# Degree-sorted neighbours, a stride-26 node layout and one maxima scheme for every head group in a two-layer graph kernel

## The chip, the cores and the metric

The kernel runs on one core of a Trainium2 chip. The core has a matrix engine (PE, with its weight loads listed as PEld), a vector engine (DVE), an activation engine (ACT), a general engine (POOL) and a queue engine (SP) that issues most of the transfers. Each works through its own instructions in order. The metric is the device time of one execution in microseconds (us); less is better.

## The reference

There are 3327 nodes with 128 features and a sparse matrix `adj` of about five entries a row, self-loops included. The second layer is the expensive one.

```python
# layer 0
x = layernorm(x + (A/rowsum(A)) @ x @ W_in + (A.T/rowsum(A.T)) @ x @ W_out)
# layer 1: N = 3327 nodes, 128 "heads" of 8 components each
q, k, v = [(x @ W.T).reshape(128, N, 8) for W in (Wq, Wk, Wv)]
a = einsum('dnh,dmh->dnm', q, k) * 128**-0.5
a = softmax(a + adj + adj, axis=2)            # 128 matrices of N x N
out = einsum('dnm,dmh->dnh', a, v)
x = layernorm(x + out.reshape(N, 1024) @ Wo.T)
```

The reshape cuts the flat row of q, k and v: head d holds the flat entries d*N to (d+1)*N.

## The kernel before

It never adds `adj` to the N x N scores. It makes a softmax without `adj` for all keys, makes the few neighbour terms apart, and joins the two at the end. Fewer than 17 entries a row have to be nonzero; a proof made on the way (`worst`, `crowd`, `short`, `outside`) decides at the end whether a general and much longer second path (`general_maxima`, `general_sums`) must run instead.

**Before the main loop.** Layer 0 reads `adj` and its transpose, and the vector engine takes each row's 16 largest entries (`weight`, `where`). Then 13 rounds of projections write q, k and v to DRAM: in three bf16 parts for the matmuls (`q_d`, `k_d`) and in f32 (`qf_d`, `kf_d`, `v_d`). The squared length of each key goes to `size_d` and that of each query to `reach_d` (ACT square, DVE reduction, L660 to L664). For the first 32 heads `early_of` selects the 2048 longest keys of a head (`select`), packs them with one-hot matmuls (`fills`, tile `hot`), and spreads them into `k_kept`.

**The main loop** goes over 32 groups of four heads (`GH`), seven blocks of up to 512 queries (the last has 255), and 26 tiles of 128 keys. A step is one key tile: two "halves" of two heads each. A half is a pair of matmuls of 50 rows, 24 key rows twice over and two rows that add the negated maximum (`e_ps`, L1241), and one exp of 128x1024 (`es`, L1259; L1261 in the last block, where one half does four heads). Each step ends with the eight f32 matmuls of four heads' weighted sums (`o`, L1192). A full group is 338 halves, 312 of them L1259.

**The side streams** are woven into these halves by a hand-written order (`tc.manual_schedule`), so that what an engine does next is fixed at build time.

- The *maxima* that a softmax needs come from `stream_of`, one "item" at a time: two matmuls into two of three PSUM banks (L1001) and two DVE reductions (L1010). Groups 1 to 31 use two levels. `of_top` takes 26 query tiles against the 1024 longest keys, 52 items for each pair of heads; `fix` finds by `reach * top_least > best**2` at most 8 queries a partition that need more, gathers them on POOL (`slot_each`, L816 to L826, then `slot_parts`); `of_rest` runs those against the next 1024 keys, 18 items; `merge` joins both. Group 0 uses `of_block`: every query against all 2048 keys, 208 items. `to_queries` transposes the result and stores it in four pieces per block (`negmax_d<-turned`, L938) and copies it to `flatmax_d` (L942).
- `due` says how many items must be out at which half; an item goes out where it is behind. 49 items (`LEAD`) go out ahead of the first half. Up to half 310 (`READY`) the rate is almost an item a half, and about one in two later.
- `choices` runs `select` for the other 96 heads, from half 310 on (DVE, L421 to L530).
- `by_node` copies k and v into tables by node (`kn_d`, `vn_d`), one transfer of 26 nodes each, every sixth half up to half 1536 (`START`).
- `neighbours` goes from half 1536 on over 26 tiles of 128 nodes (node = 128*t + p). For each of 16 slots it gathers a neighbour's k row (L1041) and takes 128 dot products on DVE (`dots`, L1076 and L1080); after an exp, 16 v rows are gathered, weighted and added on POOL (L1145, L1146). Query rows and results move in pieces of 32 nodes by SP (`transfer`, L1070). It may advance only where the estimated work of DVE and POOL (`credit`) leaves room.

The transfers of the maxima's and the exp's operands are queued in `coming` and go out on SP one per half (`begin_next`, L387); a block's own are forced out when it begins. Keys are laid out by tile and partition as t*128 + p, so that `v4`, `whole_q` and `reach_of` are loaded in pieces of 36, 32 and 4 bytes.

**After the loop** `last` joins both softmax parts, multiplies by Wo and normalizes.

Of the kernel before, what the change touches and what calls it, by code (L numbers as in the profile page):

```python
# [9 lines left out]
F32 = mybir.dt.float32  # L10
# [15 lines left out]
H = 8  # L26
# [15 lines left out]
SLOTS = 16  # L42
EPS = 1e-5
# [3 lines left out]
QUARTER = 32  # L47
STRIPE = 26
START = 1536
LEAD = 49  # L50
TURN = 5
# [16 lines left out]
READY = 310  # L68
# [12 lines left out]
def gnn_layers(ctx: ExitStack, tc: tile.TileContext, x, adj, adjt, w_in, w_out, wq, wk, wv, wo, out):  # L81
# [34 lines left out]
    near = const.tile([P, NT, SLOTS], U32, name="near")  # L116
    weight = const.tile([P, NT, SLOTS], F32, name="weight")
    gain = const.tile([P, NT, SLOTS], F32, name="gain")
# [12 lines left out]
    vn_d = dram.tile([N, HEADS * H], F32, name="vn_d")  # L131
    ones_d = dram.tile([2, NP], BF16, name="ones_d")
    x1_d = dram.tile([NP, D], F32, name="x1_d")
    size_d = dram.tile([G], F32, name="size_d")
    reach_d = dram.tile([G], F32, name="reach_d")
# [3 lines left out]
    negmax_d = dram.tile([NG * len(BLOCKS), 2, GH * NB], BF16, name="negmax_d")  # L139
# [23 lines left out]
    with ExitStack() as c0:  # L163
# [4 lines left out]
        with ExitStack() as c1:  # L168
# [14 lines left out]
            nc.gpsimd.dma_start(near_d[HEADS * N :, :].rearrange("(o g) w -> o g w", o=1), zeros)  # L183
            nc.gpsimd.dma_start(
# [3 lines left out]
            big = c1.enter_context(tc.tile_pool(name="big", bufs=1))  # L188
            rows = c1.enter_context(tc.tile_pool(name="rows", bufs=6))
# [89 lines left out]
            nc.vector.tensor_copy(near, where)  # L279
            with tc.tile_pool(name="ps_mix", bufs=2, space=PSUM) as ps_mix:  # L280
# [16 lines left out]
                nc.vector.tensor_reduce(over, used, axis=AX.X, op=ALU.add)  # L297
                nc.vector.tensor_tensor(over, over, count, op=ALU.not_equal)
                nc.vector.tensor_scalar(below, below, -1.0, 0.0, op0=ALU.mult, op1=ALU.max)
# [9 lines left out]
        early = c_att.enter_context(tc.tile_pool(name="early", bufs=1))  # L309
        hot_no = early.tile([P, 2 * REACH], BF16, name="hot_no")  # L310
# [11 lines left out]
        def load_group(g):  # L322
# [9 lines left out]
            for j in range(GH):  # L332
                at = (g * GH + j) * N
                pairs.append((v4[:, j, :, :], v_d[at : at + NP, :].rearrange("(t p) w -> p t w", p=P)))
# [13 lines left out]
        def load_queries(what, g, b):  # L348
# [5 lines left out]
            for y in range(2):  # L354
                for slot, part in enumerate(QROWS):
                    r = 64 * (y if what == "e" else 1 - y) + H * slot
                    src = q_d[part * H : (part + 1) * H, at : at + GH * N].rearrange("h (x y n) -> y h x n", y=2, n=N)[y]
                    pairs.append((q[r : r + H, :, :wp], src[:, :, :wp]))
            chunk = negmax_d[g * len(BLOCKS) + b]
            for y in range(2 if what == "e" else 0):  # L360
                pairs.append((q[64 * y + KR : 64 * y + KR + 2, :, :], chunk.rearrange("a (x y n) -> y a x n", y=2, n=NB)[y]))
# [47 lines left out]
        def select(pool, bank, first, n, tag=""):  # L409
# [11 lines left out]
            nc.sync.dma_start(sizes[: P - 1], flat[:, :whole].rearrange("h (p t) -> p h t", t=NT))  # L421
# [181 lines left out]
        with ExitStack() as c1:  # L603
# [9 lines left out]
            def early_of(first, n, g):  # L613
# [4 lines left out]
                packed = chooser.tile([P, KEPT], BF16, name="packed", bufs=2)  # L618
# [9 lines left out]
                spread(g, packed)  # L628

            choosing = [(early_of(*EARLY[0], 0), 1, 8), (early_of(*EARLY[1], 1), 4, 9)]  # L630
            for t in range(NT // 2):
# [4 lines left out]
                for s in range(2):  # L636
                    for name in ("wq", "wk", "wv"):
# [20 lines left out]
                        square = stage.tile([P, H, D], F32, name="square", bufs=1)  # L658
                        scale = 0.5 * D**-0.5 if name == "wq" else 1.0
                        nc.scalar.activation(square.rearrange("p h c -> p (h c)"), pr, AF.Square, scale=scale)  # L660
                        size = stage.tile([P, D], F32, name="size")
                        nc.vector.tensor_reduce(size, square.rearrange("p h c -> p c h"), axis=AX.X, op=ALU.add)
                        to = reach_d if name == "wq" else size_d
                        nc.gpsimd.dma_start(to[g].rearrange("(p s c) -> p s c", p=P, s=2)[:, s], size)  # L664
# [28 lines left out]
    with c_att as c1:  # L693
# [21 lines left out]
        def fills(g, at, parts):  # L715
            packed = side.tile([P, KEPT], BF16, name="packed")
            for u in range(TCUTS):
                state = {}
                tiles = tiles_of_fill(u)
                yield "hots", g, at, tiles[0], state  # L720
                for t, after in zip(tiles, [*tiles[1:], None]):
                    yield "fill", g, at, parts, packed, u, t, after, t == tiles[0], state
# [4 lines left out]
        def of_block(b):  # L727

            ntl = -(-BLOCKS[b][1] // P)
            mx = work.tile([P, NB // P, GH, KCUTS], F32, name="mx_block")  # L730
            q = queries_of("b", 0, b)
            begin_all(("b", 0, b))
            if b + 1 < len(BLOCKS):
                queries_of("b", 0, b + 1)
            for i in range(ntl):
                for x in range(2):
                    for c in range(KCUTS):
                        yield "maxima", 0, q[:, x, :], mx, i, i, x, c, 2 * x
            running.append(after_block(b, ntl, mx))

        def after_block(b, ntl, mx):
            yield
            most = work.tile([P, GH, NB // P], F32, name="most_block")
            nc.vector.tensor_reduce(
                most[:, :, :ntl], mx[:, :ntl].rearrange("p i j c -> p j i c"), axis=AX.X, op=ALU.max
            )
            two = work.tile([P, 2, GH, NB // P], BF16, name="two_block")
# [818 lines left out]
```

## Time and profile before

| | |
|---|---|
| median of 3 runs | 13527.34 us (13521.73 to 13539.56) |
| profiled execution, its own time | 13491.75 us |
| its span | 13490.0 us |
| granted PE clock, mean | 0.922 |
| busy share of the span | PE 86%, ACT 81%, DVE 73%, POOL 34% |
| first exp of the main loop, last one's end | 1080.8 us, 13226.2 us |
| DMA packets, of these under 512 bytes | 3442249, 3104237 |

A line of a group reads: source line, engine, operation, output and inputs with their shapes, count | busy time, mean duration in ns | idle time of the engine just before, and what ended it. A line of waits reads: who waited, for whom, us in all, times, longest. A line of a window reads: start and end in us, length, busy time of the engine with its number of instructions, granted PE clock, share of DMA in use, GB/s. The chain is the work that ended last, followed back. "SPq" is SP issuing a transfer; its duration holds the time that the queue made it wait.

### The profile page before, as it was taken

What the parts mean: (1) busy time and instruction counts of PE and PEld (TensorE: products, weight loads), DVE (VectorE), ACT (ScalarE), POOL (GpSimd) and SP (SyncE); (2) the same over time, 40 slices, a digit from 0 to 9 for tenths busy, and PEclk for the clock granted to TensorE, in tenths of its full rate; (3) what the DMA queues carried; (4) which work ended last, traced back from release to release, by engine and by line L of the source; (5) the groups of instructions that cost most, each with busy time, mean ns of one, the idle gap of its engine ahead of it and who ended that gap; (6) DMA issues with size and microseconds to landing.
All of it is one profiled execution on the core that took longest, in us unless ns stands there. A gap on an engine that the chain in (4) does not pass through costs nothing.

```text
span 13490.0 us, 241141 instructions
## 1 busy us (share of the span) xinstructions
PE 11609.4 (86%) x90040; PEld 2857.1 (21%) x90072; DVE 9913.6 (73%) x19323; ACT 10989.4 (81%) x11667; POOL 4541.7 (34%) x4468
## 2 busy tenths in 40 slices
PE   7558878779988889989989899988899899888985
PEld 3221112112221222222222222211222222211113
DVE  9688867667777777777777877777777777778626
ACT  6345767768988889989888899988899899888993
POOL 0120111011444334444432444333444443243454
PEclk8768989889999999999999999999999999999996
DMA  6563344433344445434443344444434444443466
GB/s 236 151 164 30 31 34 35 30 27 44 68 68 63 60 64 74 73 65 68 62 54 58 61 64 71 62 61 66 72 68 69 61 69 63 56 67 57 75 82 132
DMA packets 3442249, 949.64 MB, mean 70 GB/s; under 512 B 3104237, under 2 KB 3285989, under 8 KB 3434407
## 3 DMA queue, kind: packets, MB, share of 16 engines
q1 hardware_dynamic: 3306151, 417.22, 30.6%
q0 software_dynamic: 130176, 470.37, 12.7%
q10 hardware_dynamic: 4736, 46.52, 1.0%
q8 instruction: 710, 11.63, 0.4%
q14 instruction: 476, 3.90, 0.1%
HBM read 780.63 MB, written 156.90 MB: 69 GB/s over the span
## 4 chain that ended last, share of the span: by engine, by line
PE 36%; ACT 24%; DVE 14%; issue 10%; SPq 9%; DMA 7%; POOL 1%; ACTq 0%; DVEq 0%; POOLq 0%
ACT es L1259 21%; PE o L1192 17%; PE e_ps L1241 11%; PE m L1001 4%; SPq L387 4%; DVE mx_top L1010 3%; DVE hot L569 2%; ACT es L1261 1%; DMA reach_of<-reach_d 1%; DMA negmax_d<-turned 1%; DMA near_d<-acc 1%; SPq L777 1%; PE acc L232 1%; SPq L1070 1%; DMA k_kept<-packed 1%
## 5 line engine op out<-in xcount | busy, mean ns | idle before, releaser
L1259 ACT ACTIVATE es<-e_ps 128x1024 f32<-128x1024 f32 (+1 forms) x9984 | 9508.8, 1026 | 1492.2 <-PE e_ps L1241 1376.7
L1192 PE MATMUL o<-es,v 128*9 128x512 f32 x46592 | 5926.1, 581 | 38.1 <-ACT es L1261 9.8
L1010 DVE TENSOR_REDUCE mx_top<-m 128x1 f32<-128x512 f32 x6448 | 4128.9, 684 | 1545.6 <-PE m L1001 1474.0
L1241 PE MATMUL e_ps<-q_e,k_st 50*128 50x512 bf16 (+1 forms) x23296 | 4399.3, 378 | 293.0 <-ACT es L1259 120.3
L1241 PEld LDWEIGHTS <-k_st 50*128 50x128 bf16 (+1 forms) x23296 | 1403.8, 96 | 6893.6 <-issue 6272.2
L1001 PE MATMUL m<-k_kept,q_m 48*128 48x512 bf16 x6448 | 1387.5, 387 | 553.8 <-DMA k_kept<-packed 346.4
L1010 DVE TENSOR_REDUCE mx_rest<-m 128x1 f32<-128x512 f32 x1984 | 1273.0, 684 | 453.5 <-PE m L1001 448.0
L569 DVE TENSOR_SCALAR hot<-hot_no,at 128x336 bf16<-128x336 bf16 x3840 | 1265.0, 393 | 250.8 <-PE m L578 231.3
L1041 POOL DMA_INDIRECT near_rows<-kn_d,near x416 | 402.7, 968 | 2774.7 <-DVE prod L1076 2495.5
L816 POOL TENSOR_TENSOR slot_each<-hits,whole_q 128x832 f32<-128x832 f32 x248 | 409.1, 1650 | 2510.9 <-DVE hits L801 2061.7
L1192 PEld LDWEIGHTS o<-es,v 128*9 128x9 f32 x46592 | 696.6, 89 | 1828.7 <-issue 1477.2
L1146 POOL TENSOR_TENSOR acc<-acc,prod 128x1024 f32<-128x1024 f32 x390 | 907.6, 2327 | 30.6
L1261 ACT ACTIVATE es<-e_ps 128x1020 f32<-128x1020 f32 x832 | 832.3, 1021 | 83.9 <-PE e_ps L1241 50.9
L1145 POOL TENSOR_TENSOR prod<-near_rows,s 128x1024 f32<-128x1024 f32 x390 | 772.2, 1980 | 6.8
L1041 POOL DMA_INDIRECT near_rows<-vn_d,near x416 | 410.4, 987 | 542.2 <-DVE prod L1076 464.3
L1001 PE MATMUL m<-k_kept,slot_rows_q 48*128 48x512 bf16 x1984 | 428.5, 391 | 178.9 <-DVE mx_rest L1010 178.5
L1076 DVE TENSOR_TENSOR prod<-qn,near_rows 128x512 f32<-128x512 f32 x832 | 572.8, 692 | 3.5 <-POOL acc L1146 3.5
L1080 DVE TENSOR_REDUCE s<-prod 128x64 f32<-128x512 f32 x832 | 558.7, 675 | 0.0
L578 PE MATMUL m<-hot,parts 128*24 128x168 bf16 (+9 forms) x7200 | 327.9, 232 | 125.5 <-DVE hot L569 124.6
L1001 PEld LDWEIGHTS <-q_m 48*128 48x128 bf16 x6448 | 334.8, 98 | 395.1 <-DMA k_kept<-packed 339.0
L232 PE MATMUL acc<-a_t,x 128*128 128x512 f32 (+1 forms) x728 | 311.3, 584 | 63.9 <-DMA a_t<-in_adj_dram 43.7
L1010 DVE TENSOR_REDUCE mx_block<-m 128x1 f32<-128x512 f32 x416 | 257.0, 681 | 38.4 <-DMA q_b<-q_d 19.8
(287 smaller groups left out, 6278.8 us busy)
## 6 DMA issues: line engine op xcount, KB each, us to landing
q_m<-q_d SPq DMA_DIRECT2D x744, 52.0 KB
q_e<-q_d SPq DMA_DIRECT2D x2304, 16.0 KB
a_t<-in_adj_dram ACTq DMA_DIRECT2D x13, 1663.5 KB
a_t<-in_adj_dram SPq DMA_DIRECT2D x13, 1663.5 KB
a_t<-in_adjt_dram SPq DMA_DIRECT2D x13, 1663.5 KB
a_t<-in_adjt_dram ACTq DMA_DIRECT2D x13, 1663.5 KB
q_d<-parts SPq DMA_DIRECT2D x13, 1536.0 KB
k_d<-parts SPq DMA_DIRECT2D x13, 1536.0 KB
```

The costliest lines, as they stand in the source:

```text
L569: nc.vector.tensor_scalar(hot, hot_no, at[:, t, j : j + 1], None, op0=ALU.is_equal)
L1001: nc.tensor.matmul(banks[y], of[rows[y], i * P : (i + 1) * P], kept[rows[y], x, c * NB : (c + 1) * NB], start=True, stop=True,)
L1010: nc.vector.tensor_reduce(mx[:, n, j + y, c - c0 : c - c0 + 1], banks[y], axis=AX.X, op=ALU.max)
L1041: nc.gpsimd.indirect_dma_start(rows.rearrange("p d h -> p (d h)"), None, table, bass.IndirectOffsetOnAxis(ap=near[:, t, i : i + 1], axis=0))
L1076: nc.vector.tensor_mul(both[:, d], left[:, d], right[:, d])
L1080: nc.vector.tensor_reduce(to[:, d], both[:, d], axis=AX.X, op=ALU.add)
L1145: nc.gpsimd.tensor_mul(prod, vg, share)
L1146: nc.gpsimd.tensor_add(acc[:, :, :H], acc[:, :, :H], prod)
L1192: nc.tensor.matmul(o[32 * j : 32 * j + VW, :w], v4[:pt, j, t, :], e[j][:pt], start=t == 0, stop=t == NT - 1,)
L1241: nc.tensor.matmul(bank[:pt, y, x * NB // per : x * NB // per + w], k[r, x0 + x, t * P : t * P + pt], q[r, x0 + x, :w], start=True, stop=True,
L1259: nc.scalar.activation(es[:pt, :, :w], bank[:pt, :, :w], AF.Exp, scale=2.0)
L1261: nc.scalar.activation(es[:pt].rearrange(shape, x=per)[:, :, :, :w], bank[:pt].rearrange(shape, x=per)[:, :, :, :w], AF.Exp, scale=2.0,)
```

## The change

Neighbours: the nodes of a partition are sorted by their number of neighbours (`key`, `ranked_key`, `node`), slots and weights are regathered in that order (`info_d`), and the tile of rank t has `CAPS[t]` slots, 211 in all where there were 416. More neighbours than that count as a failed proof. Query rows are gathered by node from a table of their own (`qn_d`), results are scattered to `nn_d`, and 256 transfers turn `nn_d` into `near_d` at the end of the stream. The tables have stripes of 13 nodes, one transfer every third half, and the stream starts at half 3000.

Layout: the node of partition p and tile t is 26*p + t for `v4`, `whole_q` and the maxima, so that these are loaded and stored in one piece a partition, and the matmuls take their stationary operand with a step of 26 elements. The transposes of `to_queries` go; `merge` stores the whole group at once. `reach` is made on POOL from `whole_q` (`prepare`), and `reach_d` goes, with the squares of q.

Maxima: group 0 runs `of_top` and `of_rest` like the others, and all of its 140 items go out ahead of the first half. `fills` follow `of_top(g, 1)` directly, and `of_rest(g, 0)` comes behind them. The large load of `select` is cut into pieces of 8 heads with eight turns between them.

```diff
+CAPS = [16, 14, 12, 11, 11, 10, 10, 9, 9, 8, 8, 8, 8, 7, 7, 7, 7, 7, 6, 6, 6, 5, 5, 5, 5, 4]
-STRIPE = 26
-START = 1536
-LEAD = 49
+STRIPE = 13
+START = 3000
-READY = 310
+READY = 500
...
+                nc.vector.scalar_tensor_tensor(key[0], over, 32.0, tile_no, op0=ALU.mult, op1=ALU.subtract)
+                for r in range(0, 32, 8):
+                    nc.vector.max(ranked_key[:, r : r + 8], key[1])
+                    nc.vector.max_index(found_at[:, r : r + 8], ranked_key[:, r : r + 8], key[0])
+                    nc.vector.match_replace(key[1], ranked_key[:, r : r + 8], key[1], -1.0e9)
...
+                nc.vector.tensor_tensor(key[0], ranked_key[:, :NT], caps, op=ALU.is_gt)
+                nc.vector.tensor_add(over, over, key[0])
...
-                pairs.append((v4[:, j, :, :], v_d[at : at + NP, :].rearrange("(t p) w -> p t w", p=P)))
+                pairs.append((v4[:, j, :, :], v_d[at : at + NP, :].rearrange("(p t) w -> p t w", t=NT)))
...
-            nc.sync.dma_start(sizes[: P - 1], flat[:, :whole].rearrange("h (p t) -> p h t", t=NT))
+            for h in range(0, n, 8):
+                some = slice(h, min(h + 8, n))
+                nc.sync.dma_start(sizes[: P - 1, some], flat[some, :whole].rearrange("h (p t) -> p h t", t=NT))
+                for _ in range(8 if tag == "" else 0):
+                    yield
...
+            for t in range(NT):
+                nc.gpsimd.indirect_dma_start(
+                    info[:, t], None, info_d, bass.IndirectOffsetOnAxis(ap=node[:, t : t + 1], axis=0)
+                )
...
-                        square = stage.tile([P, H, D], F32, name="square", bufs=1)
-                        to = reach_d if name == "wq" else size_d
+                        if name == "wk":
+                            square = stage.tile([P, H, D], F32, name="square", bufs=1)
...
+        def prepare(g, x, found):
+            whole_q = side.tile([P, 2, NT, H], F32, name="whole_q", bufs=2)
+            for y in range(2):
+                nc.sync.dma_start(whole_q[:, y], qf_d[at : at + NP].rearrange("(p t) h -> p t h", t=NT))
+            for _ in range(6):
+                yield
+            nc.gpsimd.tensor_mul(squares, whole_q, whole_q)
...
-                for b in range(len(BLOCKS)):
-                    to_queries(g, b, two[:, b])
+                for a in range(2):
+                    nc.sync.dma_start(
+                        to[0, :, :whole].rearrange("j (p t) -> p j t", t=NT), two[: P - 1, a]
+                    )
+                    nc.sync.dma_start(to[:, :, whole:], two[P - 1 :, a, :, : NT - 1])
+                nc.sync.dma_start(flatmax_d[:, g * GH * N : (g + 1) * GH * N], negmax_d[g])
...
-            for b in range(5):
-                yield from of_block(b)
+            yield from of_top(0, 0)
+            yield from of_top(0, 1)
+            yield from of_rest(0, 0)
+            yield from of_rest(0, 1)
...
                 yield from of_top(g, 1)
+                    parts = split_keys(side, coming_keys[1])
+                    yield from fills(g + 1, coming_keys[0], parts)
                 yield from of_rest(g, 0)
-                    yield from fills(g + 1, coming_keys[0], parts)
                     yield from of_top(g + 1, 0)
...
+            tile_of = slice(i, NP, NT) if of.shape[-1] == NP else slice(i * P, (i + 1) * P)
-                    of[rows[y], i * P : (i + 1) * P],
+                    of[rows[y], tile_of],
...
-                for i in range(SLOTS):
+                for i in range(cap):
...
-            for _ in range(LEAD):
+            while (0, 0) not in stored:
                 for _ in next_item():
                     pass
+                taken += 1
...
-            wanted = [(0, taken), (READY, 2 * KCUTS * NT + 2 * (top + rest))]
+            wanted = [(0, taken), (2 * steps - MARGIN, taken + 4 * top + 4 * rest + 2 * fill + top)]
...
-                                        k[r, x0 + x, t * P : t * P + pt],
+                                        k[r, x0 + x, t:N:NT],
```

## The prediction

> **What bounds the kernel now.** I read the page's totals and chain first, then the windows of the exp (L1259) cut at the group boundaries, the waits, one step of PE, the SP queue, and the groups of two head groups.
>
> ```profile
> PE 11609.4 (86%) x90040; PEld 2857.1 (21%) x90072; DVE 9913.6 (73%) x19323; ACT 10989.4 (81%) x11667; POOL 4541.7 (34%) x4468
> ...
> ACT es L1259 21%; PE o L1192 17%; PE e_ps L1241 11%; PE m L1001 4%; SPq L387 4%; DVE mx_top L1010 3%; DVE hot L569 2%; ACT es L1261 1%; DMA reach_of<-reach_d 1%; DMA negmax_d<-turned 1%; DMA near_d<-acc 1%; SPq L777 1%; PE acc L232 1%; SPq L1070 1%; DMA k_kept<-packed 1%
> ```
>
> PE and ACT are both the busiest and neither is full. In the chain, the entries of SP and DMA (L387, `reach_of`, `negmax_d`, `near_d`, L777, L1070, `k_kept`) add up to some 10%: transfers hold the loop up, not one engine. The windows, with ACT's time in L1259:
>
> ```profile
> 1020.00:1080.80 60.80, 1.28 (x1) 0.50 0.04 9
> 1080.80:1972.00 891.20, 599.75 (x624) 0.95 0.42 34
> 1972.00:3317.30 1345.30, 896.02 (x936) 0.88 0.38 32
> 3317.30:12557.70 9240.40, 7421.86 (x7800) 0.95 0.43 64
> 12557.70:13226.20 668.50, 591.12 (x624) 0.99 0.60 81
> 8113.80:8464.00 350.20, 296.59 (x312) 0.98 0.48 69
> 6972.40:7370.10 397.70, 297.97 (x312) 0.91 0.37 62
> ```
>
> With 312 exps of L1259 a group, these windows hold groups 0-1, 2-4, 5-29, 30-31, then group 18 and group 15 alone. The last two groups, almost without maxima, take 334 us each: ACT paces them. The others take 446, 448 and 370. So the main loop (12,145 us) holds about 32 x 334 = 10,700 us that this change cannot touch and some 1,450 us that wait for something. From the waits, and from the queue of SP:
>
> ```profile
> PE m L1001 <- DMA k_kept<-packed: 346.4, 52, 34.0
> DVE reach_of L786 <- DMA reach_of<-reach_d: 167.5, 30, 16.1
> DVE count_of L448 <- DMA s<-no_size: 132.6, 3, 54.3
> DVE turned L935 <- DMA negmax_d<-turned: 120.0, 42, 11.7
> ...
> 475.92 7.01 SPq L422 DMA_DIRECT2D room<-size_d  x1
> 1969.38 38.41 SPq L422 DMA_DIRECT2D s<-size_d  x1
> 13200.88 28.35 SPq L1070 DMA_DIRECT2D near_d<-acc  x5
> ```
>
> A DVE or PE wait reaches ACT because both run in order: the maxima's reduction is late, its PSUM bank is not free, and the next `e_ps` stands behind that maxima matmul. The SP lines show transfers held in the queue: 38.41 us behind a load of 32x127 pieces, 7.01 behind 4x127, 28.35 for five neighbour pieces ahead of the last `o_d`.
>
> **Before the loop: -20 us.** 26 of the 52 reductions of L662 (1949 ns each) and their squares go: 51 us of DVE work, of which I take half as lying on the chain, -25. The 26 gathers of `info` cost 26 x 0.97 (the row of L1041) = 25 us of POOL, ahead of the first query copies; POOL waits for ACT there, so +5.
>
> **The lead: +187 us.** Before, 60.8 us pass from the first reductions to the first exp. Now group 0's 140 items and about 10 of group 1, during which `merge` takes its turns, come first: 150 x 2 x 684 ns (L1010) = 205 us, with ACT idle. Add 10 us of small DVE operations and 8 us for the last POOL pieces of `fix`, which mostly run beside the 18 items of `of_rest(0, 0)`. The stores of 127 partitions x 4 pieces hold SP like the 4x127 load, twice 7 us, and the queries that carry the maxima come behind them: 25 us. Together 248, less 61.
>
> **Groups 0-1: -125 us.** Group 0 took 1.37 us a half at about 0.9 items a half (565 reductions of L1010 in the 440 us from 1100 on), group 5 took 1.03 at 0.51. Now 396 items fall on 616 halves, 0.64. Between these rows that is 1.14 x 616 + 1.05 x 60 = 766 us against 891.
>
> **Groups 2-4: -135 us.** The three 32x127 loads made DVE wait 132.6 us. Cut in four, each holds SP about 9.5 us (38.4/4), eight turns apart, and DVE finds the data: -115. The other waits go as below, -20.
>
> **Groups 5-29: -480 us**, from four things.
>
> - Waits that end: `k_kept` lands behind `of_rest(g, 0)` instead of just ahead of its use, 346.4/32 = 10.8 us a group; `reach_of` becomes POOL work, 5.2; the `turned` buffers go, 3.8. About -20 a group. Their cover is the 36 halves of `of_rest` and the six turns of `prepare`; without it these 20 us are back.
> - New: the POOL work of `fix(g, 1)`, four pieces of 4.5 us (L816 to L826) and 2 us of `slot_parts`, now runs beside `fills`, and so do the 5.3 us of `split_keys` (L556 to L559). The first `fill` matmul waits for these; behind it on PE stands the next `e_ps`, and ACT behind that. DVE's `hot` suffers beside POOL:
>
> ```profile
> L569 DVE TENSOR_SCALAR hot<-hot_no,at 128x336 bf16<-128x336 bf16 x120 | 29.3, 306 | 5.9 <-PE m L578 5.4
> L569 DVE TENSOR_SCALAR hot<-hot_no,at 128x336 bf16<-128x336 bf16 x120 | 79.2, 728 | 10.0 <-PE m L578 10.0
> ```
>
> The first line is group 18, the second group 15, where the v rows' additions fell on the fills; that group is 47.5 us longer. 26 us of POOL work against the 87 us that the 52 halves of fills took there: 47.5 x 26/87 = 14 us a group. The bounds are 0 and 47. These two items leave -6 x 25 = -150.
> - Six groups like group 15 cost about 230 us over the 350 of a good one. With 211 v rows for 416 about half of that goes: -100.
> - The rest above 350 (9240 - 25 x 350 - 230 = 260 us) sits in lumps of SP: `v4` in 36-byte pieces, `near_d` and `qn` in pieces. All but the tables end: -230. The new copy to `flatmax_d` makes SP wait until the stores of `negmax_d` land, with the next `q_e` pieces queued behind it; these have a block of 50 us to come in, so I set it at nothing, and at 15 us a group if a block ends just then. What is late next is ACT itself.
>
> **Groups 30-31 and the end: -34 us.** 8 us of stalls, and the 28.35 us of neighbour pieces ahead of the last `o_d`, 26. The 256 transfers of `nn_d` are hidden: the 26 x 17 dot-product slots of before took the 26 groups from 4 to 30, so 211 + 26 take 14 to 16 groups from half 3000 (group 9), and the transfers end near group 26. If they came after the loop, each would add the 0.6 us (median) that a table transfer of L1025 holds SP, 150 us in all.
>
> **Strided stationary operands: nothing.** This is the one unknown price. Four lines of PE and one of its loads:
>
> ```profile
> 8308.11 0.39 PE L1241 MATMUL e_ps<-q_e,k_st 50*128 50x512 bf16 x2
> 8308.34 0.38 PE L1001 MATMUL m<-k_kept,q_m 48*128 48x512 bf16 x2
> 8308.76 0.39 PE L1241 MATMUL e_ps<-q_e,k_st 50*128 50x512 bf16 x2
> 8310.06 0.39 PE L1241 MATMUL e_ps<-q_e,k_st 50*128 50x512 bf16 x2
> 8308.34 0.10 PEld L1241 LDWEIGHTS <-k_st 50*128 50x128 bf16 x1
> ```
>
> A pair holds PE 0.23 us, but the second `e_ps` starts 0.42 after `m`: 0.19 us a step are free. Only the load after `o` is exposed, the other two come 0.22 or more ahead. A load of L us then costs (L - 0.10) + 2 x (L - 0.22) - 0.19 a step, which is zero up to L = 0.24. No stationary operand with such a step is in this trace. The nearest row is L662, which reads with a step of 512 bytes: 1949 ns for 1024 elements where twice L1010 is 1368, a factor 1.42. Bounds: 0.10 and 0.14 us, both hidden; I take 0.
>
> The Trainium skill ("SBUF — State Buffer", Door 1: The DMA port swizzle) speaks against this: SBUF has 16-byte lines, and each access that crosses to a new line pays, so bf16 may step at most 8 elements for free; the change steps 26. It gives no size, and no run here shows one. If it doubled the load to 0.20, the sum above would stay as it is.
>
> **The sum.** -20 + 187 - 125 - 135 - 480 - 34 = -607 us, on the profiled execution's own 13,492: 12,885. The median of the runs stands 0.26% above that execution (13,527), so 12,920.
>
> **Rivals.**
>
> - *POOL beside the fills eats the gain.* If the fills slow down in every group as in group 15, by some 30 us instead of 14, groups 5-29 give almost nothing: about 13,330, still 1.5% faster by the first five groups. For it: 728 ns. Against: `credit` keeps the neighbours out while POOL is behind.
> - *No such contention*, if POOL's pieces fall between the `hot`s: 14 x 25 = 350 us more, 12,570.
> - *Slower: the strided loads.* From L = 0.28 us, 2.8 times today's, the formula gives 0.104 us a step, and 5824 steps eat 607 us. At 0.35 it is 0.32 x 5824 = 1,860, so about 14,780. For it: two of three matmul kinds are hit. Against: the factor 1.42.
> - *The second path runs*, because a proof fails. The reference's own adjacency has 5.02 entries a row and 15 at most; sorted by partition the largest per rank are 15, 11, 10, 10, 9, 9, 8, and so on, all within CAPS. Recomputed with the new partitions, the queries that need more than `of_top` number 7 at most, and 8 fit. If it ran, it would repeat the whole loop without the two levels: at least another 12,145 us.
>
> **How the numbers follow.** A difference under 0.2% cannot be told from none here. Forecast 0.67, own range 12,650 to 13,150; POOL contention 0.13 (0.02 of it within 0.2%); no contention 0.10; strided loads 0.08; second path 0.02. So faster 0.67 + 0.11 + 0.10 = 0.88, same 0.02, slower 0.10. The range reaches down to the third case and up over the second, 12,480 to 13,350, and leaves out the slower ones.
>
> **What would show it.** Right: the first exp near 1,250 us; groups 0-1 near 1.13 us a half; `k_kept`, `reach_of` and `turned` gone from the waits; PE loads of L1241 at 0.10 to 0.14 us; no neighbour work in the last five groups; `hot` above 306 ns in every group. Wrong: PE busy all through a step with ACT waiting on `e_ps`, groups 5-29 above 365 us, or a first exp after 1,350.

## The result and the profile after

The changed kernel takes 13,889.46 us (median of 4 runs, 13,886.63 to 13,898.61) against 13,529.28 before: a ratio of 1.0267, 95% interval 1.0249 to 1.0285. It is 2.7% slower. The forecast was 12,920 us, faster. The profiled execution took 13,889.24 us, with a span of 13,887.6.

The page of the changed kernel, with the totals, four rows of the 40 slices (ACT, granted PE clock, DMA share, GB/s) and the chain by line:

```profile
PE 11829.5 (85%) x89960; PEld 3776.2 (27%) x89960; DVE 9298.0 (67%) x17819; ACT 10965.3 (79%) x11599; POOL 3414.8 (25%) x4073
...
ACT  6334888888999999998998999999997333359994
PEclk9767999999999999999999999999999676679997
DMA  6562443443311222222222222222225867851003
GB/s 238 144 158 25 37 37 35 36 37 36 36 20 31 69 66 61 65 62 54 73 60 56 66 55 62 68 56 54 59 64 31 17 17 23 17 21 21 12 7 116
...
PE o L1195 29%; PE e_ps L1244 22%; ACT es L1262 9%; SPq L1151 5%; PE m L1016 5%; DMA near_d<-nn_d 3%; DVE mx_top L1025 3%; PE m L608 1%; SPq L413 1%; DVE hot L599 1%; DVE mx_rest L1025 1%; DMA q_e<-q_d 1%; PE y L1321 1%; DMA k_kept<-packed 0%; ACT o_sb L1204 0%
```

Read the slices from the left: ACT runs at 8 to 9 tenths through most of the loop, better than before, and then drops to 3 for four slices. In the same slices the DMA engines are at 6 to 8 tenths while they move 17 to 23 GB/s, where they moved 54 to 73 GB/s at 2 tenths just before. Something keeps them busy without moving bytes. The windows of the exp (L1262), cut at the group boundaries, measure the hole:

```profile
1229.50:1966.40 736.90, 594.46 (x625) 0.99 0.41 39
1966.40:3112.30 1145.90, 894.57 (x936) 0.95 0.40 36
3112.30:10523.10 7410.80, 6252.19 (x6552) 0.98 0.24 56
10523.10:12290.10 1767.00, 595.10 (x624) 0.70 0.77 20
12290.10:12968.00 677.90, 594.10 (x625) 1.00 0.15 20
12968.00:13638.90 670.90, 590.67 (x624) 1.00 0.05 9
```

These are groups 0-1, 2-4, 5-25, 26-27, 28-29 and 30-31. Groups 26-27 take 1,767 us; the next two take 678. The waits of the changed kernel name what stood in the way, and one line each of the `nn_d` transfers and of the SP queue shows it from the other side (count, then ns min/median/max, first and last start; and start, length):

```profile
ACT es L1262 <- PE e_ps L1244: 1134.2, 680, 121.4
PE e_ps L1244 <- DMA q_e<-negmax_d: 736.9, 13, 135.0
PEld L1244 <- DMA q_e<-negmax_d: 489.1, 6, 133.5
PE e_ps L1244 <- DMA near_d<-nn_d: 242.7, 3, 121.0
PE m L1016 <- DMA k_kept<-packed: 87.6, 4, 58.9
```

```profile
L1151 SPq DMA_DIRECT2D near_d<-nn_d x256: 530/4274/11757, 10587.9 to 12296.1; - x128
```

```profile
11511.84 5.45 SPq L413 DMA_DIRECT2D q_e<-negmax_d  x2
11517.33 62.72 SPq L1151 DMA_DIRECT2D near_d<-nn_d  x11
11580.16 6.95 SPq L413 DMA_DIRECT2D k_kept<-packed  x1
```

All but the last of the 256 transfers that turn `nn_d` into `near_d` fall into groups 26 and 27, as forecast ("the transfers end near group 26"). But one holds SP for a median of 4.27 us, not 0.6; eleven in a row hold it for 62.72 us; and the negated maxima of the next block arrive up to 135 us late. The `k_kept` waits that are left all lie in this stretch too. Without the surplus of 1,767 - 682 = 1,085 us (682 is what groups 26-27 take in the first experiment) the execution would be at 12,800, near the forecast.

### The profile page after: what moved, and what is told of

Same layout as the page of the kernel before. It is cut to its first block, busy times and chain, and to the rows that moved or that the text cites. A ratio compares the mean times of both kernels' runs of the same rounds, so it can differ in the third digit from the quotient of the medians.

```text
span 13887.6 us, 238133 instructions
## 1 busy us (share of the span) xinstructions
PE 11829.5 (85%) x89960; PEld 3776.2 (27%) x89960; DVE 9298.0 (67%) x17819; ACT 10965.3 (79%) x11599; POOL 3414.8 (25%) x4073
## 4 chain that ended last, share of the span: by engine, by line
PE 58%; ACT 10%; SPq 7%; DVE 7%; issue 6%; DMA 6%; POOL 0%; ACTq 0%; another core or an unknown queue 0%; DVEq 0%; POOLq 0%
PE o L1195 29%; PE e_ps L1244 22%; ACT es L1262 9%; SPq L1151 5%; PE m L1016 5%; DMA near_d<-nn_d 3%; DVE mx_top L1025 3%; PE m L608 1%; SPq L413 1%; DVE hot L599 1%; DVE mx_rest L1025 1%; DMA q_e<-q_d 1%; PE y L1321 1%; DMA k_kept<-packed 0%; ACT o_sb L1204 0%
## 5 line engine op out<-in xcount | busy, mean ns | idle before, releaser
L1262 ACT ACTIVATE es<-e_ps 128x1024 f32<-128x1024 f32 (+1 forms) x9984 | 9521.1, 1026 | 2004.5 <-PE e_ps L1244 1134.2
L1025 DVE TENSOR_REDUCE mx_top<-m 128x1 f32<-128x512 f32 x6656 | 4263.2, 685 | 2581.4 <-PE m L1016 2466.9
L1244 PE MATMUL e_ps<-q_e,k_st 50*128 50x512 bf16 (+1 forms) x23296 | 4863.8, 413 | 1188.7 <-DMA q_e<-negmax_d 736.9
L1195 PE MATMUL o<-es,v 128*9 128x512 f32 x46592 | 5830.0, 572 | 33.3 <-ACT es L1264 11.7
L1244 PEld LDWEIGHTS <-k_st 50*128 50x128 bf16 (+1 forms) x23296 | 2198.2, 150 | 7052.2 <-issue 5862.1
L1025 DVE TENSOR_REDUCE mx_rest<-m 128x1 f32<-128x512 f32 x2048 | 1313.8, 685 | 507.7 <-PE m L1016 499.5
L1016 PE MATMUL m<-k_kept,q_m 48*128 48x512 bf16 x6656 | 1447.1, 390 | 207.6 <-DMA k_kept<-packed 87.6
L1016 PEld LDWEIGHTS <-q_m 48*128 48x128 bf16 x6656 | 594.5, 168 | 242.4 <-issue 231.7
L1066 POOL DMA_INDIRECT near_rows<-kn_d,near x211 | 201.0, 953 | 1084.2 <-DVE prod L1076 982.5
L1016 PE MATMUL m<-k_kept,slot_rows_q 48*128 48x512 bf16 x2048 | 432.8, 385 | 17.9 <-DVE mx_rest L1025 14.1
L1138 POOL TENSOR_TENSOR acc<-acc,prod 128x1024 f32<-128x1024 f32 x185 | 432.2, 2336 | 14.5
L1137 POOL TENSOR_TENSOR prod<-near_rows,s 128x1024 f32<-128x1024 f32 x185 | 366.4, 1980 | 2.5
L1009 DVE CAST slot_rows_q<-m 48x512 bf16<-48x512 f32 x256 | 176.3, 689 | 205.9 <-PE m L1000 191.8
L1066 POOL DMA_INDIRECT near_rows<-vn_d,near x211 | 206.8, 980 | 407.0 <-DVE prod L1076 365.4
L840 POOL TENSOR_TENSOR slot_each<-slot_each 128x416 f32<-128x416 f32 x256 | 288.6, 1127 | 20.1
```

What stands on the lines that cost most here:

```text
L1016: nc.tensor.matmul(banks[y], of[rows[y], tile_of], kept[rows[y], x, c * NB : (c + 1) * NB], start=True, stop=True,)
L1025: nc.vector.tensor_reduce(mx[:, i, y, c - c0 : c - c0 + 1], banks[y], axis=AX.X, op=ALU.max)
L1066: nc.gpsimd.indirect_dma_start(rows.rearrange("p d h -> p (d h)"), None, table, bass.IndirectOffsetOnAxis(ap=rows_at, axis=0))
L1138: nc.gpsimd.tensor_add(acc[:, :, :H], acc[:, :, :H], prod)
L1195: nc.tensor.matmul(o[32 * j : 32 * j + VW, :w], v4[:pt, j, t, :], e[j][:pt], start=t == 0, stop=t == NT - 1,)
L1244: nc.tensor.matmul(bank[:pt, y, x * NB // per : x * NB // per + w], k[r, x0 + x, t:N:NT], q[r, x0 + x, :w], start=True, stop=True,)
```

## The experiments

Each kernel is the changed one with the edit shown, except where it says otherwise. The theory: the 256 transfers cost 1,085 us because they move 425,856 pieces of 44 bytes (3,327 nodes x 128 heads), which the DMA engines take slowly. The rivals: their number, their bytes, their place in the kernel, and their queue.

**1. Rows of 64 bytes.**

```diff
-CW = H + 3
+CW = 16
...
-                acc = side.tile([P, HEADS, CW], F32, name="acc", bufs=2)
+                acc = side.tile([P, HEADS, CW], F32, name="acc", bufs=1)
...
+                nc.gpsimd.memset(acc[:, :, H + 3 :], 0.0)
```

> A row of nn_d and near_d is 16 numbers (64 bytes) instead of 11 (44 bytes), the five extra ones zero; acc has one buffer instead of two, for room. Theory 1, the size of the piece: in the changed kernel's profile a 44-byte piece of near_d<-nn_d takes 43 to 49 ns of a DMA engine and a 64-byte or 32-byte piece of other transfers 8 to 10 ns; the 256 last transfers fall to about 0.6 us each on SP, groups 26 and 27 take about 340 to 355 us each instead of 826 and 941, and the time is 13,889 - 1,085 = about 12,800 (12,750 to 12,900). Theory 2, the number of transfers or of pieces, transposed from node order to head order: as many as before, so the time stays at 13,850 to 13,950. Theory 3, the bytes: 64/44 as many, the time rises to 14,300.

Measured: 12,739.32 us, 0.9409 of before (0.9393 to 0.9425). The same two groups and the same transfers in this run:

```profile
10454.30:11136.80 682.50, 594.30 (x625) 0.99 0.55 64
```

```profile
L1152 SPq DMA_DIRECT2D near_d<-nn_d x256: 530/886/3082, 10520.6 to 11132.3; - x128
```

45% more bytes in as many pieces and transfers, and the hole is gone. Theory 1 holds (the time is 11 us below its range); the number of transfers and the bytes are out.

**2. The same transfers, spread out.**

```diff
-                yield
+                for _ in range(2 + n0 // STRIPE % 2):
+                    yield
```

> The same 256 transfers in the same 44-byte pieces, but one for every 2.5 steps of the work beside the loop instead of one for every step: groups 26 to 31 carry them instead of 26 and 27. Theory 1 (the pieces cost some 1,180 us of 16 DMA engines whenever they run, and stop the kernel where they come faster than the engines take them): over about five groups (1,700 us) the engines are 0.7 to 0.8 busy, the loads of negmax and q come through, groups 26 to 31 take 340 to 420 us, the time is 12,850 to 13,250. Rival (each transfer stops the loop by its own, some 4.2 us of lost time, however far apart): the time stays within 60 us of 13,889.

Measured: 13,204.37 us, 0.9752 (0.9736 to 0.9769). The window of groups 26-30:

```profile
10468.30:12628.70 2160.40, 1484.77 (x1560) 0.89 0.57 24
```

Five groups take 2,160 us instead of the 1,694 of experiment 3, a surplus of 466 instead of 1,085. The rival falls. Theory 1's upper end holds for the time, but four of the five groups take 430 to 452 us, not 340 to 420: the pieces are dear here too, and only in part covered. They are also somewhat cheaper: a packet takes 33.3 ns on average, where it takes 44.0 in the changed kernel, and the DMA engines are 0.57 busy.

**3. The same transfers, whole rows.** `near_d` is a straight copy and column H+2 is zero, so the neighbour terms reach the wrong rows: the kernel leaves out the turn from node order to head order.

```diff
-                    near_d[: HEADS * N, :].rearrange("(d n) w -> d n w", n=N)[:, n0 : n0 + n, :],
-                    nn_d[n0 : n0 + n, :].rearrange("n (d w) -> d n w", w=CW),
+                    near_d[n0 * HEADS : (n0 + n) * HEADS, :].rearrange("(n d) w -> n (d w)", d=HEADS),
+                    nn_d[n0 : n0 + n, :],
...
-                nc.gpsimd.tensor_mul(acc[:, :, H + 2], reach, least)
+                nc.gpsimd.tensor_sub(acc[:, :, H + 2], reach, reach)
```

> The 256 last transfers keep their number and their bytes, but near_d is a straight copy of nn_d in whole rows of 5,632 bytes, without the transposition to head order; column H+2 of acc is set to zero by one subtraction so that the last stage takes the same way. The output is therefore not the reference's: the neighbour part goes to the wrong rows. Theory 1 (the pieces of 44 bytes): the transfers cost some 0.3 to 0.6 us each on SP and groups 26 and 27 take 340 to 350 us; the time is 12,780 to 12,850. Rival (the number of transfers, or their place in groups 26 and 27 behind the wait for the last indirect store): 13,700 to 13,950.

Measured: 12,741.27 us, 0.9410 (0.9395 to 0.9426). The transfers and groups 26-27:

```profile
L1151 SPq DMA_DIRECT2D near_d<-nn_d x256: 468/587/1660, 10522.3 to 11124.5; - x128
```

```profile
10457.60:11139.40 681.80, 594.55 (x624) 1.00 0.23 51
```

The bytes, the place and the wait for the last indirect store are as in the changed kernel, so none of them is the cause.

**4. Where a piece begins, or how long it is.** From experiment 1, only 11 of each 16 numbers are carried over; and rows of 48 bytes.

```diff
-                    near_d[: HEADS * N, :].rearrange("(d n) w -> d n w", n=N)[:, n0 : n0 + n, :],
-                    nn_d[n0 : n0 + n, :].rearrange("n (d w) -> d n w", w=CW),
+                    near_d[: HEADS * N, :].rearrange("(d n) w -> d n w", n=N)[:, n0 : n0 + n, : H + 3],
+                    nn_d[n0 : n0 + n, :].rearrange("n (d w) -> d n w", w=CW)[:, :, : H + 3],
...
-        nc.sync.dma_start(n_t, near_d[g, :].rearrange("(p c) w -> p c w", c=D))
+        nc.sync.dma_start(n_t[:, :, : H + 3], near_d[g, : H + 3].rearrange("(p c) w -> p c w", c=D))
```

> As the run with rows of 16 numbers (12,739), but only 11 of each 16 are carried over: pieces of 44 bytes that begin at multiples of 64 bytes on both sides. Theory 'place': a 44-byte piece is dear because its ends lie anywhere, and a piece that begins at a multiple of 64 costs what a whole 64 does: groups 26 and 27 stay at 338 to 350 us, 12,720 to 12,800. Theory 'size': a piece that is no multiple of 32 or 64 bytes is dear wherever it begins: 43 to 49 ns for a piece as in the changed kernel, 13,700 to 13,850.

```diff
-CW = 16
+CW = 12
```

> Rows of 12 numbers (48 bytes, one of them zero) instead of 11 or 16. Theory 'multiples of 64 or 32 alone': 48-byte pieces cost as much as 44-byte ones, 40 to 50 ns, groups 26 and 27 together some 1,700 us, the time 13,750 to 13,900. Theory 'multiples of 16': they cost 10 ns, the time 12,720 to 12,780. In between, should 2 pieces of 4 cost (those that begin off a 64 line on either side by 16 or 48): 20 to 30 ns, 12,800 to 13,250.

Measured: 13,269.22 us, 0.9799 (0.9782 to 0.9815), and 13,587.29 us, 1.0038 (1.0024 to 1.0053). Groups 26-27 of the one and of the other:

```profile
10526.30:11560.40 1034.10, 595.18 (x624) 0.83 0.69 34
```

```profile
10526.70:12002.50 1475.80, 594.67 (x624) 0.73 0.71 25
```

Neither pure theory holds for the first, and none of the three for the second (33.8 ns, above its 20 to 30). The trace's packets say why. The table holds the packets of the transfers' own size that begin in groups 26-27 (97 to 98% of them), and the time of these groups:

| piece | begins at multiples of | mean | median | over 100 ns | groups 26-27 |
|---|---|---|---|---|---|
| 44 bytes (changed kernel) | 44 | 44.0 ns | 11 ns | 6.3%, with 75% of the time | 1,767 us |
| 48 | 48 | 33.8 | 11 | 5.1%, 68% | 1,476 |
| 44 | 64 | 22.4 | 11 | 3.2%, 50% | 1,034 |
| 64 | 64 | 11.3 | 11 | 0.04%, 0.5% | 682 |

Most pieces take 11 ns whatever their size. What is dear is a tail of a few per cent that take 100 to over 800 ns, and of these four rows only that of whole 64 bytes at multiples of 64 is without it. Both place and size count. In the run of 44 bytes of 64, some 110 us more belong to the last stage, which reads `near_d` in 44-byte pieces there (361 us from the last exp to the end instead of 249).

**5. Another queue.** The transfers are issued by POOL, not SP.

```diff
-                nc.sync.dma_start(
+                nc.gpsimd.dma_start(
                     near_d[: HEADS * N, :].rearrange("(d n) w -> d n w", n=N)[:, n0 : n0 + n, :],
```

> The changed kernel, 44-byte pieces, but the 256 last transfers are issued by POOL instead of SP. What it tells apart is where the loads of q_e and negmax_d stand still. If behind the transfers in SP's own order: they come through now; POOL takes the hold instead, some 130 transfers a group at 3.6 us = 470 us beside its own 51 us of work, and fix stands behind that; groups 26 and 27 together 1,000 to 1,100 us instead of 1,767 to 1,821, the time 13,150 to 13,300. If in the 16 DMA engines, which are 0.77 busy with the pieces: a load waits for the same pieces from whatever queue they come, and the time stays within 150 us of 13,889 to 13,952. If POOL's hold decides over fix and with it the maxima: longer than either.

Measured: 13,849.06 us, 1.0240 (1.0223 to 1.0257); groups 26-27 take 1,696 us. The waits of this run, one store of the maxima on SP (start, length), and the two busiest DMA queues of groups 26-27 (packets, MB, share of the 16 engines; q0 carries POOL's transfers):

```profile
POOL near_d L1151 <- DMA near_d<-nn_d: 1032.9, 213, 9.2
PE e_ps L1244 <- DMA q_e<-negmax_d: 837.5, 15, 188.9
```

```profile
11184.75 220.63 SPq L906 DMA_DIRECT2D negmax_d<-two_group  x1
```

```profile
q0 software_dynamic: 12720, 20.52, 72.3%
q1 hardware_dynamic: 13368, 13.54, 19.2%
```

SP has none of the 256 transfers now, and its `negmax_d` store still stands for 220.63 us, while the DMA engines are 0.92 busy. On this queue a packet holds 40 or 64 pieces (1,760 or 2,816 bytes); its time comes to 44.9 ns a piece, about the same as in the changed kernel (44.0). The time stays within 150 us of the changed kernel, as for the second theory: what is short is the engines' time, and SP's order alone is not the cause. POOL waited 1,033 us for its own transfers, and how much of the lateness came through `fix` behind them is not separated.

**6. Were they as dear before?** The kernel before the change, `near_d` with 16 numbers a row, of which 11 are stored and read.

```diff
-    near_d = dram.tile([G, CW], F32, name="near_d")
+    near_d = dram.tile([G, 16], F32, name="near_d")
...
-                nodes = near_d[: HEADS * N, :].rearrange("(d n) w -> n d w", n=N)
+                nodes = near_d[: HEADS * N, :CW].rearrange("(d n) w -> n d w", n=N)
...
-        nc.sync.dma_start(n_t, near_d[g, :].rearrange("(p c) w -> p c w", c=D))
+        nc.sync.dma_start(n_t, near_d[g, :CW].rearrange("(p c) w -> p c w", c=D))
```

> The kernel before the change, with its near_d stored in 44-byte pieces that begin every 64 bytes instead of every 44 (which halved the price of the 256 last transfers in the changed kernel). Theory 1 (before the change the same pieces were as dear, but spread over 26 groups and hidden): the mean of its stores on SP falls from 2.7 us to under 1.5 us, and the time stays within 40 us of 13,536. Rival (they took their share of each group's 20 to 30 us above the quiet pace): 13,200 to 13,450.

Measured: 13,535.34 us, ratio 1.0000 (0.9991 to 1.0010). Inside, two changes cancel. The 44-byte packets of the stores fall from a mean of 38.0 to 22.8 ns, the stores on SP from 2.72 to 2.06 us (theory 1 said under 1.5), and the loop from 12,145 to 12,048 us; but the last stage, which now reads in pieces, takes 408 us instead of 264. So the pieces were dear before the change as well, and spread over 26 groups they were mostly hidden: a price lower by two fifths is worth some 98 us there in the two profiled executions, and nearer 145 by the medians (the profiled execution before, 13,491.75 us, lies 45 below this chip's median of that kernel). In groups 26-27 of the changed kernel the halved price saves 733 us (1,767 to 1,034). Theory 1's total came true for a reason it did not name.

This run also shows on which side the price lies. Its last stage reads 425,984 pieces of 44 bytes from DRAM, at 18.5 ns on average with 0.04% over 100 ns; its stores of such pieces to DRAM take 22.8 ns with 3.7% over 100 ns, and those of the kernel before, packed end to end, 38.0 ns with 6.9%. And `vn_d<-v_d` of the changed kernel reads 32-byte pieces that begin at multiples of 36 and writes them at multiples of 32: all 32-byte packets of that kernel together take 9.5 ns, with 0.12% over 100 ns. The tail goes with writing to DRAM; reads have little or none of it.

**7. The strided stationary operand.** Only the exp's key tiles go back to side-by-side columns, and `v4`, to go with them, to 36-byte pieces, so that what is measured is the gain of the one less the cost of the other. The maxima's strided operand (`q_m`, L1016, 168 ns a load where it was 98) stays; what it costs was not tried.

```diff
-                pairs.append((v4[:, j, :, :], v_d[at : at + NP, :].rearrange("(p t) w -> p t w", t=NT)))
+                pairs.append((v4[:, j, :, :], v_d[at : at + NP, :].rearrange("(t p) w -> p t w", p=P)))
...
-                                        k[r, x0 + x, t:N:NT],
+                                        k[r, x0 + x, t * P : t * P + pt],
```

> On top of the changed kernel, the key tiles of the exponent are consecutive columns of k again (a stationary load of 128 columns side by side instead of 26 apart), and v4 is loaded by tiles again in 36-byte pieces, to go with it. Theory A (the strided load costs 13 ns of a half, from .990 us against .977 in group 31, and is seen in every quiet group): the loads of the exponent fall from 150 ns to about 96, quiet groups fall by 4 us, and the time falls by 100 to 140 us to about 13,770. Theory B (the strided load is hidden behind the matmuls, and what differs between group 31 of both is something else): the loads fall to 96 ns all the same, and the time stays within 30 us, or rises by up to 60 us for v4's 36-byte pieces (13,830 to 13,950).

Measured: 13,637.17 us, 1.0071 (1.0055 to 1.0088), 252 us below the changed kernel although its groups 26-27 are 73 us longer. (Part of the 252 may be a difference of chips; experiment 8 takes it out.) The group of the exp's loads and a quiet group (7, with the busy times of PE, PEld, DVE, ACT and POOL), first of the changed kernel:

```profile
L1244 PEld LDWEIGHTS <-k_st 50*128 50x128 bf16 (+1 forms) x23296 | 2198.2, 150 | 7052.2 <-issue 5862.1 <-DMA q_e<-negmax_d 489.1 <-DMA near_d<-nn_d 127.7
```

```profile
3831.50:4169.40 337.90, 333.51 (x2734) 104.24 (x2732) 228.31 (x441) 325.29 (x347) 51.08 (x82) 1.00 0.12 21
```

And the same two of this one:

```profile
L1244 PEld LDWEIGHTS <-k_st 50*128 50x128 bf16 (+1 forms) x23296 | 1428.3, 95 | 7441.2 <-issue 6340.1 <-DMA q_e<-negmax_d 466.6 <-DMA near_d<-nn_d 141.6
```

```profile
3807.50:4135.30 327.80, 322.10 (x2733) 80.63 (x2732) 227.31 (x441) 323.60 (x345) 51.37 (x82) 1.00 0.15 22
```

The load falls from 150 to 95 ns and the quiet group by 10 us, in which PE, 99% busy, is the pace and not ACT. Theory A had the sign and half the size (it took 4 us a group from group 31). The steps of group 7 that hold a pair `m`, 118 in each run, show where the 10 us go (mean time from the start of one pair, or of the eight `o`, to the next):

| | `e_ps` to `m` | `m` to `e_ps` | `e_ps` to `o` | `o` to `e_ps` | step |
|---|---|---|---|---|---|
| side by side (this run) | 228 ns | 373 | 329 | 979 | 1,909 |
| step of 26 (changed kernel) | 282 | 329 | 371 | 979 | 1,961 |

Both `e_ps` pairs hold PE longer, by 54 and 42 ns; the gap behind `m` gives 44 of these back; nothing is added behind `o`. 52 ns a step over 182 steps are 9.5 us.

**8. Both together, and the chips.** Experiment 1 with the edit of experiment 7.

> Rows of 16 numbers and the exponent's key tiles in consecutive columns, both together. If the two add up: the run with tiles gained 10 us in each quiet group (337.8 to 327.8), hidden in its total of -252 by groups 26 and 27, which were longer by 73; so 12,739 less 32 times 10 = about 12,415 (12,380 to 12,460). If the strided load's price was hidden where POOL works beside the fills (groups 8 to 26), some 12,550. If v4's 36-byte pieces cost again what was saved, 12,700.

Measured: 12,545.12 us, 0.9267 (0.9252 to 0.9283), faster than both kernels, but 130 above the forecast for two changes that add up. (It is the 12,550 of the second case, but by another way, as groups 8-25 show below.) Its profile and some others showed stops of PE, of 1 to 2.3 us, that nothing in the trace explains, 9 of them before group 26 here; experiments 1, 2, 3 and 7 showed none there. So the changed kernel and the kernels of experiments 1 and 8 ran again, all on one chip, without further edits.

> The changed kernel as it is, once more, beside the next two on the same chip. In the profiles taken so far two lots of runs differ by some 60 us over groups 8 to 25 though their instructions there are the same: the changed kernel (10,523 at the start of group 26) and one lot show 11 to 14 stops of PE of 1.0 to 2.3 us that nothing in the trace explains, the other lot (10,454 to 10,468) none. If these belong to the chip, the changed kernel comes out at 13,825 to 13,900, with or without the stops, and the next two with the same; if they belong to the kernel, it shows 10 to 15 of them again, whatever the others show.

> Rows of 16 numbers once more (12,739 before). If the stops belong to the chip: 12,739 without them and 12,800 with them, 1,085 +- 20 below the changed kernel on the same chip, as groups 26 and 27 say. If they belong to the kernel: 12,739 and none.

> Rows of 16 numbers and the exponent's key tiles in consecutive columns once more (12,545 in a lot with stops, where the rows alone had 12,739 in a lot without). If the two changes add up and the chip is what differed: 300 to 325 below the rows alone on the same chip, which is 12,420 to 12,440 without the stops and 12,490 to 12,550 with them. If not: 190 to 200 below.

Measured on that chip: 13,952.36 us, 1.0311 (1.0294 to 1.0328), 52 above what was expected of it; 12,805.47 us, 0.9457 (0.9441 to 0.9473); 12,547.60 us, 0.9270 (0.9254 to 0.9285). All three show such stops again (8, 5 and 6 before group 26), and 12,739 and 12,805 are the same kernel on two chips. The chip alone doesn't make them: the kernel of experiment 6 ran on this chip too and has none, and the kernel before takes 13,532 to 13,539 us on all four chips of these runs. On one chip, the 64-byte rows save 1,147 us (expected: 1,085 +- 20; groups 26-27 of the changed kernel take 1,821 us on this one) and the key tiles 258 more. The latter is between the two theories: 10 us in each quiet group, 9 in groups 8-25, but only 6 in groups 0-5, where DVE is 0.77 busy (0.69 in the quiet group) and perhaps hides the rest.

## Why the prediction was wrong

Before the loop and the lead, step by step: the first exp came at 1,229.5 us, forecast near 1,250 (+149 instead of +167). Groups 0-1 gave 154 instead of 125, groups 2-4 199 instead of 135. Near, and a little too careful.

Groups 5-29: -480 forecast, +615 measured (9,855.7 against 9,240.4). Take away the 1,085 us of the last transfers and it is -470. **The step that failed is one sentence**, on the end of the stream: "The 256 transfers of `nn_d` are hidden". The term was put at nothing, and at 150 us at worst, with each transfer at "the 0.6 us (median) that a table transfer of L1025 holds SP". The place was right, the price was not, and with it the overlap: they cost 1,085 us. With whole 64-byte pieces the same kernel takes 12,739 and 12,805 us, inside the forecast's range. The table transfers move 32-byte pieces, at a packet mean of 9.8 ns in the profile of before; these move 44-byte ones. The row of the same pieces stood in the prediction's own fence: 28.35 us on SP for the five stores of the last 127 nodes, 16,256 pieces, is 1.74 ns a piece, and 425,856 of them would have been 743 us of SP in two groups. (All 105 stores of before, 2.72 us each, sum to 286 us: the row of stores one behind another is the one that fits.) SP's measured total is 923 us, and the loss is larger still, since what waits behind is the loop's own operands. The prediction also showed the DMA share of the last two groups (0.60) without asking what filled it: 0.27 of it are 44-byte packets.

Two more terms were mis-sized, and cancel in part, so that -470 beside -480 is partly luck. *POOL beside the fills*, priced at 14 us a group, does not show in the time: in the quiet group 7, where `fix` and `split_keys` run beside the fills, `hot` takes 375 ns (306 before) and the group takes 337.9 us:

```profile
L599 DVE TENSOR_SCALAR hot<-hot_no,at 128x336 bf16<-128x336 bf16 x120 | 37.0, 375 | 17.4 <-PE m L608 17.4
```

So the 25 x 14 = 350 us did not come as priced; in groups 8-25, where the neighbours use POOL too, their part is not separated. *The strided loads*, priced at nothing, cost 10 us a quiet group, 258 us in all on one chip. The load of 150 ns is near the bound of 0.14; what failed is the formula around it. It counted the load after `o` alone as exposed, and nothing was added there; both `e_ps` pairs took longer instead, 96 ns a step together. And of its "0.19 us a step are free" 44 ns came back (experiment 7). The gap is there in the quiet group with side-by-side loads too (373 ns, where a pair of `e_ps` needs 228); why no more of it could be filled is not shown. In groups 5-29 the strided loads cost 229 us on one chip. With -350 and +229 the forecast for these groups would have been -601, so the other terms gave some 130 us less than they promised; which of them is not shown. The rule that was weighed there (the Trainium skill, "SBUF — State Buffer", Door 1: The DMA port swizzle: a step past the 16-byte line pays) was the right warning; the size is 150 ns against 95 for a step of 26 bf16.

What was right: `reach_of` and `turned` are gone from the waits, `k_kept` fell from 346.4 us to 87.6, the three large loads hold DVE for 18.7 us instead of 132.6, the neighbours ended in group 26, and the last five groups but for the transfers are quiet. Groups 30-31 and the end gave -13, not -34.

Of the rivals, the one that ended slower (strided loads) named a real cost, 258 us against its 607 at the least, at a load (150 ns) where its formula gave nothing; its sign, PE busy all through a step with ACT waiting on `e_ps`, is what the quiet groups show. The second path did not run. No rival named the transfers. That the kernel came out slower, to which the prediction gave 0.10, has a cause that none of these cases held.

## What to carry to other kernels

Price a transfer by the row with the same piece, in size and in where it begins on the side that is written, and not by one of the same form: in these runs 64-byte pieces at multiples of 64 cost a quarter of 44-byte ones packed end to end. Work that is dear but spread out looks free; before moving it all into one place, add up its engine time and set it beside the new stretch (here 425,856 packets of 38.0 ns, 1,011 us of all 16 DMA engines, for two groups of 340). And a gap on an engine is not yet free time for any instruction: of 0.19 us that were counted as free, 44 ns came back.

## What the runs showed of the hardware

- DMA between DRAM tensors in small pieces: a median of 11 ns at 44, 48 and 64 bytes, but a mean of 44.0 (packed), 33.8 (packed) and 11.3 ns (at multiples of 64). What differs is a tail, 6.3%, 5.1% and 0.04% of the packets, at 0.1 to over 0.8 us. It goes with writing to DRAM: 44-byte reads from DRAM, at multiples of 64, had 0.04% over 100 ns, and 32-byte pieces written at multiples of 32 had 0.12%. Why a piece falls into the tail was not tried. The Trainium skill ("DMA: Bandwidth & Descriptors", Specifications) says that below 512 bytes an engine reads, modifies and writes. By that alone all three sizes would pay alike; in these runs whole 64 bytes do not.
- While the loop waited, the granted clock fell to 0.70 in groups 26-27 and was back at 1.00 in group 29.
- A stationary load of 128 bf16 columns took 95 ns side by side and 150 ns with a step of 26, and the matmul behind it 369 and 409 ns in the quiet group; a step of the loop got 52 ns longer by it.
- Two chips differ by 66 us on the same kernel (12,739 and 12,805), with slower groups 8-25 (by 69 us) and some short stops of PE on one; the kernel before takes the same time on both (13,539 and 13,536). The cause stays open.

The best version found is that of experiment 8, at 12,545 and 12,548 us on two occasions.
